# A GRU scan with expert routing: x ahead of the biases, weights in whole rows, z in halves in step 0

## The chip, the core and the metric

The kernel runs on one core of a Trainium2 chip. The time is the device time of one execution in microseconds (us), the median of several executions. Before the change it is 1164.77 us (three runs, 1163.73 to 1165.15). One execution was also profiled; its own time is 1164.63 us, and the trace of it spans 1162.8 us from the first to the last instruction.

The engines are named as in the profile: PE is the matrix engine (PEld its weight loads), DVE the vector engine, ACT the scalar engine, POOL is GpSimd, SP is the sync engine. SPq, ACTq and POOLq are the queues from which these engines issue DMAs.

## What is computed

A GRU runs over 256 time steps for a batch of 16 with 512 features, starting from the state `cond_2048`. Its states go through a router with 16 experts that each choose their best 256 tokens, through one 512x512 matrix, and are added to x. All of it is float32.

```python
def cell(h, x):
    gi = x @ W_ih + b_ih
    gh = h @ W_hh + b_hh
    i_r, i_z, i_n = jnp.split(gi, 3, axis=-1)
    h_r, h_z, h_n = jnp.split(gh, 3, axis=-1)
    r = jax.nn.sigmoid(i_r + h_r)
    z = jax.nn.sigmoid(i_z + h_z)
    n = jnp.tanh(i_n + r * h_n)
    h_new = (1.0 - z) * n + z * h
    return (h_new, h_new)
...
logits = xf @ router_w + router_b
S = jax.nn.softmax(logits, axis=-1)
G, idx = jax.lax.top_k(S.T, k)
tokens = xf[idx]
out = jnp.einsum('ekh,hd->ekd', tokens, expert_w) + expert_b
weighted = G[..., None] * out
y = jnp.zeros((bs, h), dtype=x.dtype).at[idx.reshape(-1)].add(weighted.reshape(-1, h))
```

`W_ih` and `W_hh` are 512x1536 each, that is 3 MB each; a row holds the gates r, z and n side by side, 512 columns (2 KB) each.

## The kernel before

**The scan.** The loop over `s` (line 505) runs 256 steps. A step multiplies the state by `whh` (`h_part`, line 449) into accumulators in PSUM that already hold the biases and the share of x; sigmoid, product, tanh and the blend with the old state follow on ACT and DVE, and their last product, `hs` (line 590), releases the matmuls of the next step. So the steps form one serial chain. Two successive steps form a pair: the accumulators are `ra` (r and the x part of n, 256 columns), `hn` (the h part of n) and `zz` (z), in two sets for even and odd pairs. `x_part` (line 435) multiplies x of one pair by `wih`; for pairs 2 and up it is done in the loop, one pair ahead, beside the elementwise work of a step, and there the biases come in as copies on ACT (`preset_first` and `preset_rest`). Every 512-wide product is cut into four column quadrants `j`, which work side by side in the PE array, and four blocks `k` of 128 contracted rows.

**What comes before step 0.** Pairs 0 and 1 have no step ahead of them that could do their part, so it is done in a prologue (lines 475 to 492), and that is where the change lies. The order on each engine is written out by hand there:

- PE: zero all accumulators (`begin_sums`), then 22 rounds of zero matmuls into an unused bank (`keep_clock(22)`), then `biases(1)` and `biases(0)`, which add the biases to both sets of accumulators by matmuls with a row of ones, then `x_part` of pairs 0 and 1 (first r and n of both pairs, then z), `keep_clock(2)`, and then step 0.
- DVE: three copies (lines 481 to 483) take the biases out of PSUM into `bias` and `nb` for later pairs; `turn_x` turns x of pair 0 and of pair 1; lines 491 and 492 turn the first state into `hs`.
- SP and ACT queues: `wih` in three gates (r, n, z), each gate in two halves of `k`, one on each queue, so 512 KB a DMA; then `whh` in the same way (lines 278 to 281). Then SP loads x of pairs 2 and 3.
- POOL's queue: the three biases (line 288), then x of pairs 0 and 1 as eight DMAs of 16 KB in `load_pairs` (line 273), then the first state in four DMAs (line 292).

A DMA waits for a landing semaphore that it shares with an earlier DMA: each kind of queue has eight of them that are handed out in turn. The ninth DMA on POOL's queue so waits for the landing of the first, and the thirteenth of those that SP and ACT issue for that of the fifth.

In every step `h_part` is called for r and n of blocks 0 and 1, then r and n of blocks 2 and 3, then z of all four blocks (lines 508 to 511). Each of these six pieces (a gate of two blocks) is 16 matmul records.

Of the kernel before, what the change touches and what calls it, by code (L numbers as in the profile page):

```python
# [13 lines left out]
ALU = mybir.AluOpType  # L14
# [4 lines left out]
def kernel(  # L19
# [34 lines left out]
    nc = tc.nc  # L54
    B, T, D = x.shape
    E = router_w.shape[1]
    P = 128
    QD = 32
    KC = D // P
# [48 lines left out]
    def begin_sums(bank):  # L108

        n = bank.shape[-1]  # L110
        for j in range(KC):
            nc.tensor.matmul(
                bank[QD * j : QD * (j + 1)],
                zero,
                zero[:, 0:E].unsqueeze(1).to_broadcast([P, n // E, E]),
                start=True,
                stop=True,
                tile_position=(0, QD * j),
            )
# [69 lines left out]
    with (  # L189
# [9 lines left out]
        def slot(s):  # L199
            return 1 + (s - 1) % (2 * TG) if s else 0  # L200

        wih = wts.tile([P, KC, 3, D], F32, name="wih")
        whh = wts.tile([P, KC, 3, D], F32, name="whh")
        bias = wts.tile([P, 3, P], F32, name="bias")
        nb = wts.tile([P, P], F32, name="nb")
        rb = wts.tile([P, E], F32, name="rb")

        b_raw = xs[0:2, NG - 4 : NG - 1, :]
        b_n = xs[0:1, NG - 1, :]
# [7 lines left out]
        ra = [bank[:, 0 : 2 * P].rearrange("p (g d) -> p g d", d=P) for bank in banks[0:2]]  # L217
        hn = [bank[:, 0 : 2 * P] for bank in banks[2:4]]
        zz = [bank[:, 0:P] for bank in banks[4:6]]

        def quadrant(j, m=QD):
            return slice(QD * j, QD * j + m)

        def columns(ap, j):

            return ap.rearrange("p (c j i) -> p j c i", j=KC, i=QD)[:, j]

        def load_rows(dst, src, form):

            rows = src.rearrange(form, c=KC)  # L230
            for h in range(2):
                ks = slice(KC // 2 * h, KC // 2 * (h + 1))
                queues[h].dma_start(out=dst[:, ks, :], in_=rows[:, ks, :])

        xT = {}

        def load_xa(g, xa, j, qs):

            for o in range(2):
                q = QD * j + B * o  # L240
                qs[o].dma_start(
                    out=xa[q : q + B],
                    in_=x[:, g * TG + o : (g + 1) * TG : 2, j * P : (j + 1) * P],
                )
# [18 lines left out]
        queues = (nc.sync, nc.scalar)  # L263
# [3 lines left out]
        with tc.manual_schedule(engines={ET.SP, ET.Activation, ET.Pool}):  # L267
            def load_pairs(p, n, queue):

                for j in range(KC):  # L270
                    for i in range(n):
                        at = 2 * (p + i)
                        queue.dma_start(
                            out=xa0[quadrant(j), p + i, :],
                            in_=x[:, at : at + 2, j * P : (j + 1) * P].rearrange("b o d -> o b d"),
                        )

            for i, gate in enumerate((0, 2, 1)):
                load_rows(wih[:, :, i, :], w_ih[:, gate * D : (gate + 1) * D], "(p c) n -> p c n")
            for gate in (0, 2, 1):  # L280
                load_rows(whh[:, :, gate, :], w_hh[:, gate * D : (gate + 1) * D], "(c p) n -> p c n")

            for dst, src in (
                (b_raw[0:1], b_ih.rearrange("(o g d) -> o g d", o=1, d=D)),
                (b_raw[1:2], b_hh.rearrange("(o g d) -> o g d", o=1, d=D)),
                (b_n, b_hh[2 * D :].rearrange("(o d) -> o d", o=1)),
            ):
                nc.gpsimd.dma_start(out=dst, in_=src)
            load_pairs(0, 2, nc.gpsimd)
            nc.gpsimd.memset(c0, 0.0)  # L290
            for j in range(KC):
                nc.gpsimd.dma_start(
                    out=c0[QD * j : QD * j + B, :].rearrange("b (c i) -> b c i", c=KC), in_=columns(cond, j)
                )
            load_pairs(2, TG // 2 - 2, nc.sync)
            for j in range(KC):
                load_xa(1, xa1, j, (nc.sync, nc.sync))
            nc.sync.dma_start(out=ewr[:, :, E:], in_=expert_w.rearrange("(c p) n -> p c n", c=KC))
            nc.sync.dma_start(out=ewr[:, :, 0:E], in_=router_w.rearrange("(c p) n -> p c n", c=KC))
            nc.sync.dma_start(out=rb, in_=router_b.rearrange("(o e) -> o e", o=1).to_broadcast([P, E]))  # L300
            nc.sync.dma_start(out=eb, in_=expert_b.rearrange("(o d) -> o d", o=1).to_broadcast([P, D]))

        def biases(i):
            for dst, rows in (
                (ra[i][:, 0, :], b_raw[:, 0, :]),
                (ra[i][:, 1, :], b_raw[0:1, 2, :]),
                (hn[i][:, 0:P], b_n),
                (zz[i], b_raw[:, 1, :]),  # L310
            ):
                for j in range(KC):
                    nc.tensor.matmul(
                        dst[quadrant(j)],
                        ones[0 : rows.shape[0]],
                        columns(rows, j),
                        start=False,
                        stop=True,
                        tile_position=(0, QD * j),
                        skip_group_check=True,  # L320
                    )
# [3 lines left out]
        def of_step(ap, odd):  # L325
            return ap.rearrange("p (c q b) -> p c q b", q=2, b=B)[:, :, odd, :]
# [108 lines left out]
        def x_part(p, k, z):  # L435
            g, pair = divmod(p, TG // 2)
            lhs = xT[g][:, pair, QD * k : QD * (k + 1)]
            for j in range(KC):
                q = quadrant(j)
                dst, rhs = (  # L440
                    (zz[p % 2][q], columns(wih[:, k, 2, :], j))
                    if z
                    else (ra[p % 2][q], columns(wih[:, k, 0:2, :].rearrange("p g d -> p (g d)"), j))
                )
                nc.tensor.matmul(  # L445
                    dst, lhs, rhs, start=False, stop=(k == KC - 1), tile_position=(0, QD * j), skip_group_check=True
                )

        def h_part(s, gate, ks):
            p, odd = divmod(s, 2)  # L450
            m = QD if odd else B
            dst, gate_ = {"r": (ra[p % 2][:, 0, :], 0), "z": (zz[p % 2], 1), "n": (hn[p % 2][:, 0:P], 2)}[gate]
            for k in ks:


                lhs = hs[:, k, slot(s) - odd : slot(s) + 1, :].rearrange("p t b -> p (t b)")
                for j in range(KC):
                    nc.tensor.matmul(  # L458
                        dst[quadrant(j, m)],
                        lhs,  # L460
                        columns(whh[:, k, gate_, :], j),
                        start=False,
                        stop=(k == KC - 1),
                        tile_position=(0, QD * j),
                        skip_group_check=True,
                    )

        idle = ps_m.tile([P, D], F32, name="idle", tag="pe")

        def keep_clock(n):  # L470

            for _ in range(n):
                begin_sums(idle)

        with tc.manual_schedule(engines={ET.PE, ET.DVE}):
            for bank in banks:
                begin_sums(bank)
            keep_clock(22)
            biases(1)
            biases(0)  # L480
            nc.vector.tensor_copy(bias[:, 0:2, :], ra[1])
            nc.vector.tensor_copy(nb, hn[1][:, 0:P])
            nc.vector.tensor_copy(bias[:, 2, :], zz[1])
            for pair in range(2):
                turn_x(0, xa0, slice(pair, pair + 1))
            for z in (False, True):
                for pair in range(2):
                    for k in range(KC):
                        x_part(pair, k, z)
            keep_clock(2)  # L490
            nc.vector.transpose(turned, c0)
            nc.vector.tensor_copy(hs[:, :, 0, :], of_step(turned, 0))
        make_masks()
# [6 lines left out]
        with tc.manual_schedule(engines={ET.PE, ET.Activation, ET.DVE, ET.Pool, ET.SP}):  # L500
# [4 lines left out]
            for s in range(T):  # L505
                p, odd = divmod(s, 2)
                g, c = divmod(s, TG)
                for ks in (first, second):
                    h_part(s, "r", ks)
                    h_part(s, "n", ks)  # L510
                h_part(s, "z", range(KC))

# [98 lines left out]
                elif g + 2 < NG:  # L613
                    if c == KC:
                        xa_next = new_xa()
                    j = c - KC
# [22 lines left out]
    with (  # L639
# [86 lines left out]
        with tc.manual_schedule(engines={ET.PE, ET.Activation, ET.DVE}):  # L726
# [42 lines left out]
            gate = gate_of(pg)  # L769
# [3 lines left out]
            for i, (g, cols) in enumerate(items):  # L773
# [4 lines left out]
                if step == 1:  # L778
                    n = ps_n.tile([P, 1], F32, name="n", tag="n")
# [14 lines left out]
        with tc.If(again > 0):  # L794
# [53 lines left out]
            gate = gate_of(pg)  # L848
# [39 lines left out]
```

## Time and profile before

| | |
|---|---|
| median of three runs | 1164.77 us |
| profiled execution, its time and its span | 1164.63 us, 1162.8 us |
| PE busy over the span | 1147.7 us (99%) |
| DVE, ACT, POOL busy over the span | 703.6, 336.1, 100.0 us |
| first matmul of step 0 / of step 1 / of step 2 | 23.70 / 27.73 / 31.68 us |
| matmuls of step 0: 96 records | 2.79 us |
| PE busy in 0 to 23.70 us, granted clock there | 18.76 us, 0.86 |
| moved by the DMA engines in 0 to 23.70 us | 279 GB/s on the mean |

All times of single instructions below are counted from the start of the span. The change touches only what lies before and in step 0, and one operand of `x_part`; from step 1 on the kernel's instructions are the same. A shift of the start of step 1 is carried through the serial chain to the end.

A line of the timeline gives the start, the stretch from there to the end of the last instruction in that row, the engine, the line of the kernel, the operation with its output and input, and how many there are. In brackets stands how long the engine had been idle and what ended it. A line of the windows gives a stretch, its length, the busy time of PE, PEld, DVE, ACT and POOL with the number of instructions, the granted PE clock as a share of full speed, the busy share of the DMA engines, and GB/s.

### The profile page before, as it was taken

The numbers are of one execution on the slowest core, as the hardware profiler recorded it, in microseconds if no ns is written. First come the engines' busy times: TensorE is split into PE (matmuls) and PEld (weight loads), VectorE is DVE, ScalarE is ACT, GpSimd is POOL, SyncE is SP. The second block draws the span as 40 slices with busy tenths as digits, with TensorE's granted clock in tenths as the row PEclk, the third lists the DMA queues.
The fourth block names the chain that finished last, engine by engine and source line by source line (L and its number), as shares of the span: only waits on it lengthen the run. The fifth ranks groups of instructions, "written<-read, shape, count | busy, mean of one in ns | idle before, by whom it ended". The sixth has DMA issues, their size and how long they took to land. (4 is left out here: it accounts for less than half of the span.)

```text
span 1162.8 us, 79365 instructions
## 1 busy us (share of the span) xinstructions
PE 1147.7 (99%) x36025; PEld 1018.4 (88%) x36025; DVE 703.6 (61%) x4078; ACT 336.1 (29%) x1444; POOL 100.0 (9%) x412
## 2 busy tenths in 40 slices
PE   7999999999999999999999999999999999999998
PEld 4899999999999999999999999999999999989742
DVE  1656665666666666666665666666656666665675
ACT  0323223232323232323232322332223222243320
POOL 3000010000000000000000000000000000000000
PEclk8999999999999999999999999999999999999999
DMA  7200000000000000000000000000000000000017
GB/s 231 76 23 20 21 18 22 21 19 19 20 21 20 21 20 21 20 21 21 20 20 21 21 20 18 22 21 20 18 23 20 21 18 23 20 16 14 3 54 240
DMA packets 48854, 38.01 MB, mean 33 GB/s; under 512 B 7968, under 2 KB 40800, under 8 KB 48512
## 3 DMA queue, kind: packets, MB, share of 16 engines
q1 hardware_dynamic: 46272, 29.56, 8.7%
q8 instruction: 283, 4.64, 1.6%
q10 hardware_dynamic: 1632, 3.15, 0.8%
q14 instruction: 59, 0.48, 0.1%
q0 software_dynamic: 608, 0.19, 0.1%
HBM read 24.47 MB, written 8.39 MB: 28 GB/s over the span
## 5 line engine op out<-in xcount | busy, mean ns | idle before, releaser
L458 PE MATMUL gates<-whh,hs 128*16 128x128 f32 x24576 | 723.2, 273 | 3.4 <-DVE hs L590 3.3
L458 PEld LDWEIGHTS gates<-whh,hs 128*16 128x16 f32 x24576 | 675.6, 103 | 9.5 <-DVE hs L590 4.1
L445 PE MATMUL gates<-wih,xt 128*32 128x256 f32 (+1 forms) x8192 | 385.7, 327 | 4.0 <-DVE xt L258 4.0
L445 PEld LDWEIGHTS gates<-wih,xt 128*32 128x32 f32 x8192 | 256.0, 110 | 65.9 <-DVE xt L258 4.3
L516 ACT ACTIVATE r<-gates 128x128 f32<-128x128 f32 x256 | 71.1, 278 | 614.1 <-PE gates L458 614.1
L520 DVE COPY seen<-r 1x1 f32<-1x1 f32 x256 | 36.3, 142 | 330.2 <-ACT r L516 330.2
L569 ACT ACTIVATE t<-t 128x64 f32<-128x64 f32 x512 | 102.9, 248 | 131.6 <-DVE t L567 131.6
L576 DVE STREAM_TRANSPOSE nT<-t 128x64 f32<-128x64 f32 x512 | 100.3, 234 | 49.0 <-ACT t L569 49.0
L579 DVE STREAM_TRANSPOSE zT<-zs 128x64 f32<-128x64 f32 x512 | 121.6, 237 | 0.2 <-issue 0.2
L590 DVE TENSOR_TENSOR hs<-v,nT 128x32 f32<-128x32 f32 x512 | 101.6, 198 | 21.7
L587 DVE TENSOR_TENSOR v<-u,zT 128x32 f32<-128x32 f32 x512 | 104.5, 204 | 8.8
L407 PE MATMUL pe<-ewr,ht 128*32 128x128 f32 x1920 | 97.0, 273 | 0.0
L565 DVE TENSOR_TENSOR t<-r,gates 128x64 f32<-128x64 f32 x512 | 89.7, 217 | 0.0
L567 DVE TENSOR_TENSOR t<-t,gates 128x64 f32<-128x64 f32 x512 | 88.4, 214 | 0.0
L407 PEld LDWEIGHTS pe<-ewr,ht 128*32 128x32 f32 x1920 | 63.6, 110 | 17.4
L582 DVE TENSOR_TENSOR u<-hs,nT 128x32 f32<-128x32 f32 x512 | 78.3, 153 | 0.0
L570 ACT ACTIVATE zs<-gates 128x128 f32<-128x128 f32 x256 | 71.0, 277 | 0.0
L137 PE MATMUL pe<-ewr,ht 128*32 128x256 f32 (+1 forms) x848 | 64.5, 442 | 0.5 <-ACT pe L160 0.5
L617 POOL COPY xa<-hs 32x1 f32<-32x1 f32 x120 | 21.4, 179 | 478.2 <-DVE hs L590 297.4
L333 POOL COPY ht<-hs 128x128 f32<-128x128 f32 (+1 forms) x128 | 46.8, 396 | 160.9 <-DVE hs L590 153.1
L249 POOL COPY xs<-hs 1x1 f32<-1x1 f32 x128 | 22.7, 178 | 338.5 <-DVE hs L590 333.5
L137 PEld LDWEIGHTS pe<-ewr,ht 128*32 128x32 f32 x848 | 25.9, 109 | 27.0 <-issue 16.8
(102 smaller groups left out, 310.1 us busy)
## 6 DMA issues: line engine op xcount, KB each, us to landing
xs<-in_x_dram SPq DMA_DIRECT2D x128, 64.0 KB
xa<-in_x_dram SPq DMA_DIRECT2D x248, 32.0 KB
out_dram<-xs SPq DMA_DIRECT2D x31, 256.0 KB
wih<-in_L_cond_W_ih_dram SPq DMA_DIRECT2D x3, 512.0 KB
wih<-in_L_cond_W_ih_dram ACTq DMA_DIRECT2D x3, 512.0 KB
whh<-in_L_cond_W_hh_dram SPq DMA_DIRECT2D x3, 512.0 KB
whh<-in_L_cond_W_hh_dram ACTq DMA_DIRECT2D x3, 512.0 KB
ewr<-in_L_ffn_expert_w_dram SPq DMA_DIRECT2D x1, 1024.0 KB
```

Source lines behind the costliest of these rows:

```text
L137: nc.tensor.matmul(pe[q, cols], ht[:, g, k, q], ewr[:, k, E:][:, cols], start=False, stop=(k == KC - 1), tile_position=(0, QD * j), skip_g ...
L407: nc.tensor.matmul(pes[g][quadrant(j), at : at + P], ht[:, g, k, quadrant(j)], ewr[:, k, E + P * quarter : E + P * (quarter + 1)], start=( ...
L445: nc.tensor.matmul(dst, lhs, rhs, start=False, stop=(k == KC - 1), tile_position=(0, QD * j), skip_group_check=True)
L458: nc.tensor.matmul(dst[quadrant(j, m)], lhs, columns(whh[:, k, gate_, :], j), start=False, stop=(k == KC - 1), tile_position=(0, QD * j), ...
L565: nc.vector.tensor_tensor(t[half], r[:, cols], hn[p % 2][:, cols], ALU.mult)
L567: nc.vector.tensor_tensor(t[half], t[half], ra[p % 2][:, 1, cols], ALU.add)
L569: nc.scalar.activation(t[half], t[half], AF.Tanh)
L576: nc.vector.transpose(nT[half], t[half])
L579: nc.vector.transpose(zT[half], zs[:, halves[half][1]])
L582: nc.vector.tensor_tensor(u[half], hs[:, halves[half][2], slot(s), :], of_step(nT[half], odd), ALU.subtract)
L587: nc.vector.tensor_tensor(v[half], u[half], of_step(zT[half], odd), ALU.mult)
L590: nc.vector.tensor_tensor(hs[:, halves[half][2], slot(s + 1), :], v[half], of_step(nT[half], odd), ALU.add)
```

## The change

- On POOL's queue the eight loads of x of pairs 0 and 1 go ahead of the three biases.
- `wih` is loaded in two DMAs instead of six: blocks 0 and 1 (all three gates, 1.5 MB) on SP's queue, blocks 2 and 3 on ACT's. `whh` is loaded in four DMAs instead of six, one for each block of 128 rows (768 KB), by turns on SP and ACT. In SBUF `wih` now holds the gates in the order of the matrix (r, z, n), so `x_part` reads r and n with a gap between them.
- `biases` runs once, after `x_part` and `keep_clock(2)`, into the unused bank `idle`. DVE copies it to `bias` and `nb`; then, for each of the two pairs, ACT copies `nb` to `hn` and DVE adds `bias` to `ra` and to `zz`. Only then come the two DVE instructions that turn the first state.
- In step 0 z is done in two halves: r, n, z of blocks 0 and 1, then r, n, z of blocks 2 and 3.

```diff
-            for i, gate in enumerate((0, 2, 1)):
-                load_rows(wih[:, :, i, :], w_ih[:, gate * D : (gate + 1) * D], "(p c) n -> p c n")
-            for gate in (0, 2, 1):
-                load_rows(whh[:, :, gate, :], w_hh[:, gate * D : (gate + 1) * D], "(c p) n -> p c n")
-
+
+            rows = w_ih.rearrange("(p c) (g n) -> p c g n", c=KC, g=3)
+            for h in range(2):
+                ks = slice(KC // 2 * h, KC // 2 * (h + 1))
+                queues[h].dma_start(out=wih[:, ks], in_=rows[:, ks])
+            for k in range(KC):
+                queues[k % 2].dma_start(
+                    out=whh[:, k], in_=w_hh[k * P : (k + 1) * P, :].rearrange("p (g n) -> p g n", g=3)
+                )
+
+            load_pairs(0, 2, nc.gpsimd)
...
-            load_pairs(0, 2, nc.gpsimd)
...
-        def biases(i):
-            for dst, rows in (
-                (ra[i][:, 0, :], b_raw[:, 0, :]),
-                (ra[i][:, 1, :], b_raw[0:1, 2, :]),
-                (hn[i][:, 0:P], b_n),
-                (zz[i], b_raw[:, 1, :]),
-            ):
+        def biases(bank):
+
+            for i, rows in enumerate((b_raw[:, 0, :], b_raw[0:1, 2, :], b_raw[:, 1, :], b_n)):
                 for j in range(KC):
                     nc.tensor.matmul(
-                        dst[quadrant(j)],
+                        bank[quadrant(j), P * i : P * (i + 1)],
...
-                    (zz[p % 2][q], columns(wih[:, k, 2, :], j))
+                    (zz[p % 2][q], columns(wih[:, k, 1, :], j))
                     if z
-                    else (ra[p % 2][q], columns(wih[:, k, 0:2, :].rearrange("p g d -> p (g d)"), j))
+                    else (
+                        ra[p % 2][q].rearrange("p g (c i) -> p g c i", c=KC),
+                        wih[:, k, 0:3:2, :].rearrange("p g (c j i) -> p j g c i", j=KC, i=QD)[:, j],
+                    )
...
             keep_clock(22)
-            biases(1)
-            biases(0)
-            nc.vector.tensor_copy(bias[:, 0:2, :], ra[1])
-            nc.vector.tensor_copy(nb, hn[1][:, 0:P])
-            nc.vector.tensor_copy(bias[:, 2, :], zz[1])
...
             keep_clock(2)
+            biases(idle)
+
+            nc.vector.tensor_copy(bias, idle[:, 0 : 3 * P].rearrange("p (g d) -> p g d", d=P))
+            nc.vector.tensor_copy(nb, idle[:, 3 * P :])
+            for pair in range(2):
+                nc.scalar.copy(hn[pair][:, 0:P], nb)
+                nc.vector.tensor_tensor(ra[pair], ra[pair], bias[:, 0:2, :], ALU.add)
+                nc.vector.tensor_tensor(zz[pair], zz[pair], bias[:, 2, :], ALU.add)
             nc.vector.transpose(turned, c0)
...
                     h_part(s, "r", ks)
                     h_part(s, "n", ks)
-                h_part(s, "z", range(KC))
+                    if s == 0:
+                        h_part(s, "z", ks)
+                if s:
+                    h_part(s, "z", range(KC))
```

More of the change, by code (lines that the diff above doesn't have):

```diff
@@ L226, in columns @@
             return ap.rearrange("p (c j i) -> p j c i", j=KC, i=QD)[:, j]
[L228 to L233, printed above, removed]
         xT = {}
```

## The prediction

> **What bounds the kernel now.** I read the page first. Its PE row has one dip, in the first of the forty slices of 29 us, and PEclk and DMA show that this slice differs in the clock and in the transfers too:
>
> ```profile
> PE   7999999999999999999999999999999999999998
> PEclk8999999999999999999999999999999999999999
> DMA  7200000000000000000000000000000000000017
> ```
>
> The diff touches this slice and nothing else but an operand of x_part. So the question is when step 0 starts and when it ends. The timeline of the first 26 us answers what it waits for now:
>
> ```profile
> 9.89 1.96 PE L313 MATMUL gates<-xs,ones 2*32 2x128 f32 x64
> ...
> 15.42 0.40 DVE L258 STREAM_TRANSPOSE xt<-xa 128x128 f32<-128x128 f32 x1 [4.00 <-DMA xs<-in_cond_dram]
> 15.88 7.56 PE L445 MATMUL gates<-wih,xt 128*32 128x256 f32 x128 [4.03 <-DVE xt L258]
> ...
> 18.25 0.20 DVE L492 COPY hs<-nT 128x64 f32<-128x64 f32 x1
> ...
> 23.26 0.61 PE L112 MATMUL idle<-zero 128*32 128x512 bf16 x8
> ...
> 23.70 2.79 PE L458 MATMUL gates<-whh,hs 128*16 128x128 f32 x96
> ```
>
> PE does the biases at 9.89, stands still for 4.03 us, and starts x_part at 15.88, released by the turn of x at 15.42. The label of that wait names the first state's DMA. I take the last load of x instead: POOL's queue shows it.
>
> ```profile
> 7.06 0.59 POOL L273 DMA_DIRECT2D xa<-in_x_dram  x1 [1.12 <-DMA xs<-in_L_cond_b_ih_dram]
> 8.65 1.18 POOL L273 DMA_DIRECT2D xa<-in_x_dram  x2 [1.00 <-DMA xs<-in_L_cond_b_hh_dram]
> ...
> DMA to landing us min/median/max: 6.4/6.7/7.9
> ```
>
> The load issued at 8.65 is the seventh of eight, the last one of pair 0; 8.65 + 6.7 = 15.35, just ahead of the turn. From 15.88 PE is never idle until step 0's own products end, so x_part is the chain, then the two rounds of zeros (23.26 to 23.70), then step 0. The first state was ready at 18.45, over 5 us early.
>
> x_part is slow besides. The windows show the clock:
>
> ```profile
> 13.00:13.50 0.50, 0.00 (x0) 0.00 (x0) 0.00 (x0) 0.00 (x0) 0.49 (x2) 0.97 1.10 354
> 13.50:14.00 0.50, 0.00 (x0) 0.00 (x0) 0.00 (x0) 0.00 (x0) 0.00 (x0) 0.50 1.07 308
> ...
> 20.00:20.50 0.50, 0.50 (x12) 0.25 (x8) 0.00 (x0) 0.00 (x0) 0.00 (x0) 0.70 1.00 363
> 20.50:21.00 0.50, 0.50 (x16) 0.30 (x12) 0.00 (x0) 0.00 (x0) 0.00 (x0) 1.00 0.66 215
> ```
>
> In the idle stretch the clock falls to 0.50, and comes back near 20.2, after 4.3 us of x_part. Half of that, 2.15 us, is what the cold clock cost: in full clock x_part needs about 7.38 - 2.15 = 5.2 us.
>
> One more view decides: SP's own waits.
>
> ```profile
> SPq L273 <- DMA wih<-in_L_cond_W_ih_dram: 5.2, 1, 5.2
> ```
>
> SP ends its last issue for whh at 2.27 + 6.90 = 9.17 us and then stands 5.2 us until a DMA of wih has landed. By the turn of the eight semaphores that is the fifth weight DMA, SP's share of the last gate (z). So **the third megabyte of wih is there at 14.4 us**. That is no harm today: z's part of x comes last, near 21.5.
>
> **The change part by part.**
>
> *x ahead of the biases.* The eight issues take 0.6 us each and now start at 1.33 instead of 2.93. They are the first eight of the queue, so both waits (1.12 and 1.00) leave them. Pair 0's last load, the seventh, is issued at 1.33 + 6 x 0.61 = 5.0 and lands 6.7 later: 11.7 (11.4 to 12.9 by the row's ends). With 0.46 from turn to matmul, x alone would let x_part start at 12.2, 3.7 us sooner. The biases go out as ninth to eleventh after x's first landing (1.33 + 6.7 = 8.0), by about 10, and land by 16.5. The first state's four loads are issued by about 12.5 and land by 19. Both are hidden behind x_part, which ends no sooner than 17; each would cost directly if more than 5 us later.
>
> *wih by whole rows.* x_part of block 0 now needs all three gates of blocks 0 and 1, and block 2 half a microsecond later those of the other DMA. The first 2 MB no longer suffice. The bytes ahead in the queues are the same 3 MB whose last part landed at 14.4, and x's loads, which lie beside it, are all within this time now. From below: all bytes that the DMA engines moved (windows of 5 us: 187, 353 and 326 GB/s) reach the 3.1 MB of wih and 0.13 of x at about 12.0. From above: 14.4, or a microsecond later. I take the measured 14.4, so x_part starts at **14.5**; 1.4 us are won here, not 3.7. The range keeps 12.2.
>
> PE then idles from 9.96, the end of keep_clock(22), to 14.5, 4.5 us against 4.03 now, so I leave x_part its cold clock and its 7.4 us: it ends at 21.9, against 23.26.
>
> *Biases into the idle bank.* Gone are 64 records (1.96 us) from a place where PE waited afterwards: gain nothing. Added, behind x_part and the two rounds (0.44): 32 records, half of 1.96, 0.98 us. Then DVE, in order. These rows price it:
>
> ```profile
> L419 DVE TENSOR_TENSOR ht<-pe,eb 128x256 f32<-128x256 f32 x28 | 11.7, 418 | 0.0
> L481 DVE COPY bias<-gates 128x256 f32<-128x256 f32 x1 | 0.4, 425 | 9.7 <-PE gates L313 9.7
> L482 DVE COPY nb<-gates 128x128 f32<-128x128 f32 x1 | 0.3, 281 | 0.0
> ```
>
> The three bias copies start at 10.60, 10.94 and 11.14, so the next instruction starts 0.34 after one of 256 and 0.20 after one of 128. The new copy of 384 is 0.49, nb 0.20. An add in PSUM is not in the trace for these shapes; by L419 it costs what a copy of its width does: 2 x (0.34 + 0.20) = 1.08. Then the turn of the state (17.90 to 18.25, 0.35), its copy 0.20, and 0.15 until PE (as from hs at 27.58 to 27.73). Sum **2.47 us**, all on the chain, since no matmul of step 0 can start without hs and hs is behind it in DVE's order. ACT's two copies to hn (0.27 each) run beside the adds. ACT's table load (1.28 us, now at 10.10) may slip behind them; it would still be over before r is due, 2 us after step 0 starts. The DVE work for the masks (18.36 to 19.4 now) slips into step 0's first 2 us, where DVE waits for r; put ahead of hs it would cost 1.1.
>
> So step 0 starts at 21.9 + 0.44 + 0.98 + 2.47 = 25.8 instead of 23.70: **+2.1**.
>
> *z in halves.* In step 0 r's second half now has z's first half ahead of it, a sixth of 2.79: r is **0.47 later**, and with it n and the state. It would pay only if blocks 2 and 3 of whh were not there yet. But the DMA rate falls from 363 to 68 GB/s by 21.5: the weights are through well before 25.8. So whh in row blocks brings nothing either.
>
> *A second idle stretch.* While DVE works, PE waits 2.5 us. No stretch of that length is in the trace: 1.2 us within steps 0 and 1 keep the clock, the 4.03 us lost it. A rule is to be weighed here: the Trainium skill (TensorE: Matmul & The Clock Gate, Why this matters for your kernels) warns only of gaps above some 3 us. By it 2.5 us cost nothing. The row speaks for caution: the clock fell at 13.3, only 1.5 us after the last bias matmul, so those matmuls with one or two rows hardly counted as work, and the stretch is then 3.5 us. If the clock falls, some 3.4 us of step 0 run at half speed (an estimate from the two changes near 13.35 and 20.2, twice 3.4 apart): 1.7 us. By the rule the change makes +2.6, by the row +4.3; I take half, **+0.8**.
>
> *The gap in wih.* x_part's 256 columns are eight runs of 32 as before, with another stride between the fourth and fifth. I take no cost; a slower read would hit every pair.
>
> Sum: 2.1 + 0.47 + 0.8 = +3.4 on the profiled 1164.63, **1168.0 us**. The median before, 1164.77, stands 0.14 above the profiled run. This case reaches from +1.7 to +5.2 (no or full loss at the second stretch, wih a microsecond either way): 1166.3 to 1169.8.
>
> SP has three weight DMAs instead of six, and so reaches x of pairs 2 and 3 sooner; they are needed at 32.4, and are issued by 24.3 now.
>
> **Rivals.**
>
> *x decides, wih is in time (faster).* With rows of 6 KB the transfers may be more even and wih there by 12. x_part starts at 12.2 after 2.2 us of idle PE. If this keeps the clock, 5.2 us lead to 17.4, and 0.44 + 0.98 + 2.47 to 21.3; with 0.47 the shift is -1.9: 1162.7. x at the lower end gives -2.3, and faster transfers of x more, to -3.5. If the clock falls at either stretch it is back at no change. For it: 400 GB/s at 4 to 7 us, before x's small loads begin. Against: the 14.4.
>
> *x starves behind long rows (slower still).* The Trainium skill (DMA: Bandwidth & Descriptors, Queues, rings and completion order) says that a DMA engine goes round its queues packet by packet. Now SP and ACT send runs of 2 KB, and x lands in 6.7. If runs become 6 or 12 KB and a run is one turn, x's 512-byte rows wait three to six times as long. From x at 14.0 on this decides; at the worst x lands when the weights are through, 20.8. Midway, at 17, x_part starts at 17.5: three more, 1171.0. For it: landing already takes 5.4 to 7.9 us beside the weights. Against: the loads' latencies hardly grow from first to last, so turns are short now.
>
> *x_part slower in all pairs.* r and n of x take 16 groups of 0.21 us for two pairs, about 106 us over 62 pairs; 10% more is +10, 1175.
>
> **How the numbers follow.** A difference below 0.2% (2.3 us) can't be told from none here, so faster is below 1162.4, slower above 1167.1. My forecast has 0.50, of which 0.40 slower and 0.10 same; x deciding 0.30 (0.17 faster, 0.13 same); starving 0.17 and x_part slower 0.03, both slower. Faster 0.17, same 0.23, slower 0.60. The range runs from 1161.8, where about 0.1 is left out below, to 1172.5, with another 0.1 above.
>
> **What would show it.** In the profile after: the first x_part near 14.5 (at 12.2 wih was in time; past 17 x starved), with the turn of x ended by 12.2 all the same; a DVE stretch of 2.4 us between the bias matmuls and step 0 with PE idle; step 0 starting at 25.8, r 2.0 after it; the clock at 0.5 or 1.0 in step 0. It is wrong if wih lands by 12, if PE stays warm in both stretches, or if the 256-column matmuls of later pairs take longer than now.

## The result and the profile after

The changed kernel takes 1176.38 us (median of four runs, 1175.0 to 1176.94) against 1164.96 us of the kernel before beside it: a ratio of 1.0099, with a 95% interval of 1.0087 to 1.0111. It is **slower by 11.4 us**, and lies above the top of the predicted range, 1172.5. The profiled execution took 1176.77 us, its span is 1174.9 us.

The page of the changed kernel shows the loss in the first slice, and now in part of the second:

```profile
PE   5799999999999999999999999999999999999998
PEclk7999999999999999999999999999999999999999
DMA  6200000000000000000000000000000000000017
```

The timeline of the changed kernel, with the rows that answer to those of before:

```profile
20.38 0.40 DVE L251 STREAM_TRANSPOSE xt<-xa 128x128 f32<-128x128 f32 x1 [19.48 <-DMA xs<-in_L_cond_b_ih_dram]
20.84 8.11 PE L440 MATMUL gates<-wih,xt 128*32 128x256 f32 x128 [11.23 <-DVE xt L251]
28.77 0.61 PE L112 MATMUL idle<-zero 128*32 128x512 bf16 x8
29.31 1.08 PE L305 MATMUL idle<-xs,ones 2*32 2x128 f32 x32
30.46 0.56 DVE L483 COPY bias<-idle 128x384 f32<-128x384 f32 x1 [8.41 <-PE idle L305]
...
32.53 0.20 DVE L490 COPY hs<-nT 128x64 f32<-128x64 f32 x1
32.78 4.48 PE L453 MATMUL gates<-whh,hs 128*16 128x128 f32 x96 [2.38 <-DVE hs L490]
...
38.92 2.83 PE L453 MATMUL gates<-whh,hs 128*32 128x128 f32 x96 [1.66 <-DVE zT L580]
```

PE stands still for 11.23 us instead of 4.03, and again the turn of x ends the wait: at 20.38 instead of 15.42, though x was issued sooner. (The label of the turn's own wait names a bias's DMA; the last load of pair 0 landed at 20.25.) Behind x_part come the bias matmuls, 2.3 us of DVE work with PE idle, and a step 0 whose 96 matmuls take 4.48 us instead of 2.79.

Why x is late stands in two places. The first is the row of x's eight loads, issue to landing, min, median and max (6.4, 6.7 and 7.9 before). The second is the page's row of ACT's queue: its packets, megabytes and share.

```profile
DMA to landing us min/median/max: 8.0/12.9/15.9
...
q10 hardware_dynamic: 432, 3.15, 0.7%
```

ACT's queue moves nothing but its half of the weights. Before, the same 3.15 MB were 1632 packets; now they are 432. Of these 48 signal the ends of three DMAs, and 384 carry data: 128 of 12 KB (two rows of `wih`) and 256 of 6 KB (a row of `whh`). Beside such runs a 16 KB load of x needs nearly twice as long to land, and the median hides that the wait grows from load to load: the seventh, the last one of pair 0, was issued at 5.1 and needed 15.2 us. `wih` itself came sooner. SP's third load of x for the later pairs shares its semaphore with SP's half of `wih`, and waited for it until 11.4 (3.7 + 7.7); the fourth shares that of ACT's half, and did not have to wait for it:

```profile
SPq L266 <- DMA wih<-in_L_cond_W_ih_dram: 7.7, 1, 7.7
```

The windows of the changed kernel show when the clock came back in x_part, and that it fell a second time:

```profile
26.00:26.50 0.50, 0.50 (x12) 0.28 (x8) 0.00 (x0) 0.00 (x0) 0.00 (x0) 0.64 0.00 0
...
32.75:33.25 0.50, 0.47 (x16) 0.46 (x20) 0.46 (x4) 0.48 (x3) 0.18 (x1) 0.94 0.00 0
33.50:36.50 3.00, 3.00 (x64) 2.62 (x60) 0.18 (x2) 1.14 (x2) 0.00 (x0) 0.50 0.09 27
```

A mean of 0.64 over half a microsecond puts the return at 26.36, 5.5 us after x_part's start; before it was at 20.30, 4.4 us after (0.70 in 20.00 to 20.50).

The start of step 1 moves from 27.73 to 38.92, by 11.19 us:

| term | before | after | shift |
|---|---|---|---|
| first x_part | 15.88 | 20.84 | +4.96 |
| x_part to the end of its stretch | 7.38 | 7.93 | +0.55 |
| zeros, biases, DVE, until step 0 | 0.44 | 4.01 | +3.57 |
| step 0, first matmul to that of step 1 | 4.03 | 6.14 | +2.11 |

Between steps 4 and 5, counted at the start of r, another 1.45 us are lost. The waits of PE in the changed kernel, 20 to 60 us, name it, with no releaser:

```profile
PE gates L453 <- issue: 1.1, 1, 1.1
```

Later steps win 0.35 back in all. So there are five losses to be told apart: x late, the clock, the bias chain, z in halves, and that stall, which is called the stall in step 5 below.

### The profile page after: what moved, and what is told of

Its sections match the earlier page's. It is cut to its first block, busy times and chain, and to the rows that moved or that the text cites. A ratio compares the mean times of both kernels' runs of the same rounds, so it can differ in the third digit from the quotient of the medians.

```text
span 1174.9 us, 79299 instructions
## 1 busy us (share of the span) xinstructions
PE 1149.0 (98%) x35993; PEld 1017.5 (87%) x35993; DVE 703.8 (60%) x4081; ACT 338.0 (29%) x1447; POOL 99.6 (8%) x412
## 3 DMA queue, kind: packets, MB, share of 16 engines
q10 hardware_dynamic: 432, 3.15, 0.7%
## 5 line engine op out<-in xcount | busy, mean ns | idle before, releaser
L399 PEld LDWEIGHTS pe<-ewr,ht 128*32 128x32 f32 x1920 | 63.4, 110 | 17.7
L251 DVE STREAM_TRANSPOSE xt<-xa 128x512 f32<-128x512 f32 (+2 forms) x34 | 37.2, 1095 | 27.0 <-DMA xs<-in_L_cond_b_ih_dram 19.5
```

Source lines behind the costliest of these rows:

```text
L399: nc.tensor.matmul(pes[g][quadrant(j), at : at + P], ht[:, g, k, quadrant(j)], ewr[:, k, E + P * quarter : E + P * (quarter + 1)], start=( ...
```

## The experiments

The shift in the table below is that of the start of step 1 against before, in the profiled execution. x_part's start is that of its first matmul.

| kernel | x, median to landing | x_part starts | shift at step 1 | time and ratio to before |
|---|---|---|---|---|
| before | 6.7 | 15.88 | 0 | 1164.1 to 1165.1 in the four groups of runs |
| changed | 12.9 | 20.84 | +11.19 | 1176.38, 1.0099 (1.0087 to 1.0111) |
| gates_x_first | 7.1 | 13.38 | +2.98 | 1169.69, 1.0039 (1.0025 to 1.0054) |
| short_runs | 7.1 | 12.94 | +4.20 | 1176.16, 1.0096 (1.0079 to 1.0113) |
| six_kb_rows | 11.1 | 18.89 | +8.61 | 1174.1, 1.0092 (1.0077 to 1.0108) |
| rows_only | 12.3 | 22.02 | +6.41 | 1170.9, 1.0054 (1.0037 to 1.0071) |
| x_first_only | 6.9 | 19.13 | +3.37 | 1169.05, 1.0044 (1.0028 to 1.0059) |
| warm_gaps | 13.2 | 20.96 | +6.95 | 1172.46, 1.0062 (1.0045 to 1.0079) |

### Which part makes x late

**gates_x_first** is the changed kernel with the weight loads of before:

```diff
-            rows = w_ih.rearrange("(p c) (g n) -> p c g n", c=KC, g=3)
...
+            for gate in (0, 2, 1):
+                load_rows(wih[:, :, gate, :], w_ih[:, gate * D : (gate + 1) * D], "(p c) n -> p c n")
+            for gate in (0, 2, 1):
+                load_rows(whh[:, :, gate, :], w_hh[:, gate * D : (gate + 1) * D], "(c p) n -> p c n")
```

> Everything of the changed kernel but its weight loads, which are the gate-wise ones of before (512 KB a DMA, runs of 2 KB). Long runs starve x: with 2 KB runs x of pairs 0 and 1 lands about 6.7 us after its issue, x_part starts near 12.2 instead of 20.84; with the biases' 3.5 us behind x_part and one or two clock losses still there, step 0 starts at 21.5 to 24, and the time is 1163 to 1167. Rival, the place in the queue (eight loads of x issued in a row slow each other): x still lands after about 12.9 us, x_part starts near 20, 1175 to 1177.

Its row of landings:

```profile
DMA to landing us min/median/max: 6.9/7.1/8.1
```

x lands after 7.1 us and x_part starts at 13.38. So the place at the head of POOL's queue does not slow x; the weight loads do. The time, 1169.69, is above what was expected: x_part starts 1.2 us later than was taken, and the stall in step 5 (here 1.97 us from step 4 to 5) was not counted. The biases' chain and a cold step 0 stay.

**short_runs** keeps the six weight DMAs, their sizes and their order, and changes only where they land, so that a run ends after one gate:

```diff
-        wih = wts.tile([P, KC, 3, D], F32, name="wih")
-        whh = wts.tile([P, KC, 3, D], F32, name="whh")
+        wih = wts.tile([P, KC, 3, D + 1], F32, name="wih")[:, :, :, 0:D]
+        whh = wts.tile([P, 3, KC, D], F32, name="whh").rearrange("p g k d -> p k g d")
```

> The changed kernel with the same six weight DMAs in the same order and of the same size, but SBUF layouts that keep a run from going on past one gate of one row, so all runs are 2 KB. Long runs starve x: x lands after 6 to 8 us, x_part starts when wih is complete or x is turned, 12 to 15, the time falls to 1166 to 1171. Rival, the 6 MB issued at once with no wait in between fill the DMA engines' queues ahead of x, whatever the run: x lands after 11 us or more and the time stays within 2 us of 1176.4.

```profile
DMA to landing us min/median/max: 6.7/7.1/8.3
```

x lands after 7.1 us again, with all 6 MB issued within 3.2 us. So it is the length of the runs that makes x late, not how much is queued at once. The total missed what was expected, and looks like the rival's, 1176.16: but at step 1 this kernel is 7 us ahead of the changed one, and it loses them through the whole loop, 0.02 to 0.03 us in every step. That is the price of the new layouts, told below.

Here a wait for the weights also shows: x_part's first matmuls at 12.94 were followed by a wait of 0.83 us for the second half of `wih`, which landed at 15.4. With runs of 2 KB the whole-row order is late by about what the prediction had taken.

**six_kb_rows** takes alternate rows of `wih`, so that a run is one row:

```diff
-                ks = slice(KC // 2 * h, KC // 2 * (h + 1))
-                queues[h].dma_start(out=wih[:, ks], in_=rows[:, ks])
+                queues[h].dma_start(out=wih[:, h::2], in_=rows[:, h::2])
```

> The changed kernel with the two halves of wih taken as rows 0 and 2 and rows 1 and 3 of each partition's four, so that a run is one row of 6 KB instead of two (12 KB); sizes, order and SBUF layout stay. If x waits its turn behind runs of the other two queues, landing lies between the 7.1 us of 2 KB runs and the 12.9 of 12 KB: 8.5 to 11.5 on the median, the turn of x at 15 to 18.5, and the time 1171 to 1174.5. Rival, anything above one gate's 2 KB is equally bad: 12 us or more and 1176.

```profile
DMA to landing us min/median/max: 6.7/11.1/14.4
```

The median goes 7.1, 11.1, 12.9 for runs of 2, 6 and 12 KB in `wih` (`whh` has 6 KB in the last two). The turn of x is at 18.43, at the late end of what was expected. Landing grows with the run while bytes, order and issue stay.

**rows_only** puts the whole-row loads alone (with the reading of `wih` that goes with them) into the kernel before, with its biases in front.

> The kernel before with the whole-row weight loads alone (biases first, in front of x_part; z whole). Long runs starve x: x is issued later than in the changed kernel and lands when the weights are through, about 20 to 21; x_part starts 4.5 to 6 us later than before; no second idle stretch and no DVE chain, so 1169 to 1172. Rival, the place in the queue: x lands as before, x_part starts near 15.9 or sooner, 1163 to 1165.5.

x lands 12.3 us after its issue on the median, x_part starts at 22.02, 6.1 us later than before, and the time is 1170.9. The bias chain and the second cold stretch are absent: step 0's matmuls take 2.79 us and step 1 starts 4.03 after step 0, as before.

**x_first_only** moves x ahead of the biases in the kernel before and changes nothing else.

> The kernel before with x ahead of the biases in POOL's queue and nothing else changed, so the bias matmuls still stand in front of x_part. x is turned near 12.9 as with the gate-wise loads, but the last bias is issued near 10.1 and lands near 16.5; PE does the biases there, and x_part starts at 18 to 18.5 instead of 15.9: 1166.5 to 1168. So by itself the move gains nothing, and the biases must go behind x_part. Rival, the biases land sooner than x did (6 us after issue or less): x_part starts before 16 and the time is 1163 to 1165.

The timeline of x_first_only:

```profile
15.56 3.64 PE L313 MATMUL gates<-xs,ones 2*32 2x128 f32 x64 [5.56 <-DMA xs<-in_L_cond_b_hh_dram]
...
19.13 7.68 PE L445 MATMUL gates<-wih,xt 128*32 128x256 f32 x128
```

Now the bias matmuls stand in front of x_part and wait until 15.56; they run at half the clock (3.64 us instead of 1.96). The time, 1169.05, is a microsecond above what was expected, for that reason. The move needs another place for the biases.

### The clock and z in halves

**warm_gaps** fills both idle stretches of the changed kernel with matmuls of zeros:

```diff
-            keep_clock(22)
+            keep_clock(73)
...
             nc.vector.tensor_copy(nb, idle[:, 3 * P :])
+            keep_clock(7)
```

> The changed kernel with zero matmuls into the unused bank across both idle stretches of PE: 73 rounds instead of 22 ahead of x_part, and 7 rounds behind the bias copies. The clock: x_part takes 5.2 to 5.6 us instead of 7.9 and step 0's matmuls 2.8 instead of 4.5; 1172 (1171 to 1173). Rival, x_part and step 0 are slow for another reason (operand reads or late weights): less than 1 us is won.

The timeline of warm_gaps:

```profile
20.96 5.41 PE L440 MATMUL gates<-wih,xt 128*32 128x256 f32 x128 [0.50 <-DVE xt L251]
...
30.21 2.81 PE L453 MATMUL gates<-whh,hs 128*16 128x128 f32 x96
```

x_part takes 5.41 us in place of 8.11, and step 0's matmuls 2.81 in place of 4.48; the median falls by 3.9 us. The clock was worth that much, the cold x_part that the kernel before has too included. **z_whole_warm** is the same kernel with z of step 0 in one piece:

> The kernel with both idle stretches filled (1172.46), with z of step 0 in one piece again, behind r and n. If z's first half only stands in r's way, r of step 0 comes 0.47 us sooner after the first matmul (2.00 to 1.53) and step 1 starts 0.47 sooner: 1172.0. Rival, the second half of the state's weights is late and z's first half fills that wait: r is not sooner, the time is the same or longer.

The starts of step 0 and of r in z_whole_warm, then that of r in warm_gaps, where step 0 starts at 30.21:

```profile
30.41 2.81 PE L453 MATMUL gates<-whh,hs 128*16 128x128 f32 x96
...
32.00 0.28 ACT L515 ACTIVATE r<-gates 128x128 f32<-128x128 f32 x1
...
32.21 0.28 ACT L518 ACTIVATE r<-gates 128x128 f32<-128x128 f32 x1 [0.42 <-PE gates L453]
```

r comes 1.59 us after the first matmul instead of 2.00, and step 1 starts 4.03 after step 0 instead of 4.47. So z in halves costs 0.44. On the total it can't be seen (1172.67 against 1172.46): the 0.4 us is less than the runs' spread. Of step 0's +2.11 the clock has the rest, 1.67.

### The stall in step 5

Every kernel above whose biases come behind x_part shows it; rows_only and x_first_only, with as many PE instructions ahead of the loop as before, don't. **fetch_shift** adds eight rounds (64 PE instructions) to the changed kernel, where PE waits for x anyway; **fetch_shift_before** takes eight rounds from the kernel before.

```diff
-            keep_clock(22)
+            keep_clock(30)
```

> The changed kernel with 30 rounds of keep_clock instead of 22: 64 PE instructions more ahead of the loop (as many as the two bias calls of before had more than the one call now), at a place where PE waits for x anyway. If the 1.1 us in which PE stands in step 5 with no releaser is a late fetch of instructions, whose place in the step follows the count of instructions ahead of it, it goes: step 6 starts about 1.3 us sooner after step 4, and the time is 1175.0. Rival, the stall comes from DMA traffic of that moment (the expert weights load 5 us earlier): it stays, 1176.4.

> The kernel before with 14 rounds of keep_clock instead of 22, so with 64 PE instructions less ahead of the loop, as in the changed kernel. The place of the fetch: step 5 shows a PE stall of 1 us or more which before does not have, and the time is 1165 to 1166.5. Rival, DMA traffic: no stall, the time of before.

The waits of PE in fetch_shift_before, 20 to 60 us:

```profile
PE gates L458 <- DVE zT L579: 1.2, 1, 1.2
PE gates L458 <- DVE hs L590: 1.1, 1, 1.1
PE gates L458 <- issue: 1.1, 1, 1.1
```

The third row is the stall, now in a kernel that issues the same transfers as before. From step 4 to 5 it falls back by 1.45 us, as much as the changed kernel; its time is 1165.55, 1.0011 (1.0004 to 1.0018). In fetch_shift no such wait is left, but less came back than was expected: step 6 starts 0.5 us sooner after step 4 than in the changed kernel, not 1.3, and its time is 1175.47, against 1175.0. Its steps 5 and 6 are still 0.9 us slower than before's, and why stays open.

So the number of PE instructions ahead bears on the stall. The packets of the instruction queue say more. The first row is from the page of the changed kernel, the second from its timeline:

```profile
q8 instruction: 283, 4.64, 1.6%
...
56.45 2.48 PE L453 MATMUL gates<-whh,hs 128*32 128x128 f32 x82 [1.08 <-issue]
```

A packet of this queue is 16 KB. With 71986 matmuls and weight loads on the page, some 254 of them come to a packet (an estimate from these two figures, as if the queue served PE alone). Counted in matmuls and weight loads from the start of the trace, the stall falls at about number 1722 in the changed kernel, gates_x_first, short_runs, six_kb_rows, fetch_shift_before and x_pool_bias_hw (below), and at about 2234 in the two warm kernels: 512 later, two packets. In each of these eight a packet of the queue ends 1.1 to 1.5 us before PE goes on. The kernel before and rows_only come to the same number 1.4 and 1.6 us after the end of its packet, and don't wait. So a late fetch of instructions fits in place and in time. The rival, the loads of the expert weights, does not: gates_x_first issues them 0.7 us later in its loop than before, and stalls longest. What sets the time of the fetch no run shows.

### A version from both

**x_pool_bias_hw** has the gate-wise weights and the direct bias matmuls of before, x at the head of POOL's queue (pair 0 whole, then pair 1), and the biases on SP's and ACT's queues:

```diff
             for i, gate in enumerate((0, 2, 1)):
                 load_rows(wih[:, :, i, :], w_ih[:, gate * D : (gate + 1) * D], "(p c) n -> p c n")
+                if i == 0:
+                    nc.sync.dma_start(out=b_raw[0:1], in_=b_ih.rearrange("(o g d) -> o g d", o=1, d=D))
+                    nc.scalar.dma_start(out=b_raw[1:2], in_=b_hh.rearrange("(o g d) -> o g d", o=1, d=D))
+                    nc.sync.dma_start(out=b_n, in_=b_hh[2 * D :].rearrange("(o d) -> o d", o=1))
...
-            keep_clock(22)
+            keep_clock(10)
             biases(1)
             biases(0)
+            keep_clock(9)
```

> A kernel from both: gate-wise weights in 2 KB runs and biases by matmul straight into the accumulators as before; x at the head of POOL's queue, pair 0 whole ahead of pair 1; the three biases on SP's and ACT's queues behind the first gate of wih; keep_clock split in 10 rounds ahead of the biases and 9 behind. Biases land near 6 to 8 us, x of pair 0 is turned near 10.5, x_part runs warm from about 11.2 and ends near 17; then step 0 waits for whh, whose gates land at 17 (r), 19.5 (n) and 22 (z): step 1 starts at 24 to 25.5 instead of 27.73, 1161 to 1163. Rival, x in front of POOL's queue slows the weights by as much as it gains, or step 0 only waits for z of whh until 24 or later: 1163.5 to 1165.

x is turned at 9.97, x_part runs warm from 11.08, and then PE waits for weights: 0.98 us for z of `wih`, 0.42, 1.92 and 0.44 for `whh`. Step 1 starts at 25.32, 2.41 us sooner; 0.67 of it goes in step 5. The time is 1163.24, just above what was expected, and the ratio 0.9996 (0.9987 to 1.0004): no difference that can be told.

**whh_rows_x_early** adds to it the change's row blocks for `whh` and z in halves, and three rounds, which restore the count of PE instructions.

> The kernel x_pool_bias_hw with two parts of the change added where x has already landed: whh in four row blocks with runs of 6 KB, and z of step 0 in halves; wih stays in gates with runs of 2 KB. 12 rounds instead of 9 behind the biases, so that PE has as many instructions ahead of the loop as before. x lands as in x_pool_bias_hw (6.5 us), blocks 0 and 1 of whh near 17.5 and blocks 2 and 3 near 20.5; r of step 0 near 21.3, step 1 starts at 23.6 to 24.5 (25.32 there, 27.73 before), no stall in step 5: 1160 to 1161.8. Rival, the weights land no sooner in longer runs, or the split order lets r wait for the last block until 22.5: 1162 to 1164.

Its timeline:

```profile
11.75 3.89 PE L446 MATMUL gates<-wih,xt 128*32 128x256 f32 x64
...
17.24 1.95 PE L446 MATMUL gates<-wih,xt 128*32 128x128 f32 x64 [1.60 <-DMA wih<-in_L_cond_W_ih_dram]
...
21.08 1.50 PE L459 MATMUL gates<-whh,hs 128*16 128x128 f32 x48 [1.45 <-DMA whh<-in_L_cond_W_hh_dram]
22.75 1.50 PE L459 MATMUL gates<-whh,hs 128*16 128x128 f32 x48 [0.17 <-DMA whh<-in_L_cond_W_hh_dram]
```

The two pieces of 48 are blocks 0 and 1, then 2 and 3. Each starts when its rows have landed. So the split has a wait to fill here, but it wins nothing by it. The start of r in x_pool_bias_hw, whose `whh` comes by gates, and in whh_rows_x_early:

```profile
22.21 0.28 ACT L516 ACTIVATE r<-gates 128x128 f32<-128x128 f32 x1 [13.49 <-PE gates L457]
...
23.45 0.28 ACT L521 ACTIVATE r<-gates 128x128 f32<-128x128 f32 x1 [15.21 <-PE gates L459]
```

r comes 1.2 us later than with gates, and step 1 starts at 25.91: 1.81 us sooner than before, but 0.59 later than in x_pool_bias_hw, and later than expected. z of `wih` lands later too (17.2 against 15.7). There is no stall in step 5, where x_pool_bias_hw loses 0.67. The time, 1162.67, lies in the range of the rival, not in the expected one. With a ratio of 0.9985 (0.9978 to 0.9992) the kernel is 0.15% faster than before; its interval overlaps that of x_pool_bias_hw, so no gain from the row blocks is shown.

## Why the prediction was wrong

- **The failed step is the start of x_part.** The prediction took "the measured 14.4, so x_part starts at 14.5", with x itself ready at 12.2. It started at 20.84: 4.96 us were lost where 1.4 were to be won. That the change is slower was right because of the bias chain and step 0; the largest term had the wrong sign. Both terms were wrong, and in opposite ways. `wih` was there at 11.4: long runs move faster (in 5 to 10 us the DMA engines moved 421 GB/s with runs of 12 KB, 390 in six_kb_rows, 333 in short_runs and 353 before). x was turned at 20.38, because the landing of 6.7 us was carried over from a kernel whose weights came in 2 KB runs. The rival that starves x had the mechanism and got 0.17; the midway value of 17 for x was too low, and its worst case, "x lands when the weights are through, 20.8", is what came: the last packet of the weights ended at 20.7. By the prediction's own sum that case gives some 1174.8 (an estimate: 1168.0, and 6.8 us more until x_part), which its range left out. What the prediction held against it, latencies that hardly grow, was a property of the short runs that the change takes away. The rule it cited (the Trainium skill, DMA: Bandwidth & Descriptors, Queues, rings and completion order: turns by packets) fits the 7.1, 11.1 and 12.9; what makes up one turn no run shows.
- **The bias chain was right.** Predicted 0.98 + 2.47 behind the zeros; measured 3.47 (29.31 to 32.78). The adds in PSUM took 0.42 and 0.29, as the copies of their width.
- **The second idle stretch was mis-sized.** Taken as +0.8, half of a full loss; measured 1.67, the full loss. The page on the clock that the prediction cited (the Trainium skill, TensorE: Matmul & The Clock Gate, Why this matters for your kernels) warns of gaps above some 3 us; PE was idle for only 2.38, and the clock was lost. The prediction's other reading fits: with the bias matmuls counted as idle the stretch is 3.47 us (29.31 to 32.78). The clock went from 1.00 to 0.50 at 33.2, 2.8 us after the last bias matmul.
- **x_part was left as slow as before**, and took 0.55 more: it ran 1.1 us longer at half the clock (5.5 against 4.4).
- **z in halves** was right: 0.47 predicted, 0.44 measured. "whh in row blocks brings nothing" was right as well, and no run shows a gain from them once x is early.
- **The gap in wih cost nothing:** from step 18 on the changed kernel falls no further behind.
- **The stall in step 5 was not foreseen**, +1.45. No term of the sum counted instructions that are removed as a loss.

With 4.96 for x in place of the predicted gain of 1.4, 0.55 for x_part, 3.57 for the biases, 2.11 for step 0, 1.45 for the stall and -0.35 later, the sum is 12.3 us; the profiled spans differ by 12.1.

## What to carry to other kernels

A small load's time to land is no constant of its queue: it depends on the length of the runs that the other queues have in flight. Before large loads are merged into longer rows, look for small ones that must land beside them, and get these down first. That long rows then pay for what comes later is not shown here. When work is put on a serial path, count the idle time that it gives the matrix engine as well, and look at a step well behind the change before the difference is put down to the change itself.

## What was not expected of the hardware

- **Layout in SBUF.** In short_runs a row stride of 513 elements in `wih` and a gate-major `whh` made every step slower: the shift against before grows from 5.35 us at step 18 to 11.15 at step 255. The 256-column matmuls of x_part take 385 ns on the mean against 382. Which of the two layouts does it wasn't tried.
- **The clock changes on a grid.** In the changed kernel it falls at 12.71, returns at 26.36, falls at 33.19 and returns at 36.60: the distances, 13.65, 6.83 and 3.41 us, are four, two and one times 3.41. The changes in the other traces are such multiples apart too. In all eight traces where x_part starts cold and runs without a break, the clock returns at the second of these points after its start, 3.9 to 5.7 us later; so where the start falls between two points decides part of the cost.
- **Matmuls with one or two rows hardly count for the clock.** In x_first_only PE is busy without a break from 15.56 on, first with 64 bias matmuls, then from 19.13 with x_part. The points there are 16.95, 20.37 and 23.78, and the clock returns only at 23.78, the second one after the start of x_part and not of the biases.
- **Fewer instructions can cost time.** 64 PE instructions less, all from a wait, cost the kernel before 0.11% (0.04 to 0.18).
